# A graph layer of the SAGE kind: gathering rows that are already multiplied by the weights

## The chip, the cores and the metric

One core of one Trainium2 chip runs the whole program. The metric is device time in microseconds (us). The kernel before takes 2383.64 us, the median of 3 runs (2382.04 to 2386.07).

## The reference

Four graph layers follow one another on x, 3327 nodes by 512 features, with one adjacency matrix `adj` (0 or 1). Layers 0, 2 and 3 are graph attention; layer 1 is of the SAGE kind. In front of each layer stands a layer norm and a ReLU, and its result is added to x.

```python
h = jnp.maximum(_layernorm(x, axis=-1), 0.0)
x = x + L1(h, adj, ...)
# L1:
mask = (adj > 0).astype(x.dtype)
deg = jnp.sum(mask, axis=1, keepdims=True)
agg = mask @ x / jnp.maximum(deg, 1.0)
self_f = x @ W_self + b_self
nb_f = agg @ W_nb + b_nb
out = jnp.concatenate([self_f, nb_f], axis=-1) @ W_comb + b_comb
return relu(out)
```

The adjacency is sparse, and nodes of low number have many more neighbours than those of high number (the chance of an edge falls with the root of both numbers).

Layer 1 can be written as relu(h Ws + (mask h / deg) Wn + b), where Ws and Wn are the two weights already multiplied with the halves of W_comb, and b is the sum of the biases. Both kernels compute Ws, Wn and b beside layer 0, and use them (`Wx[:, 0]` and `Wx[:, 1]`, `bias`).

## The kernel before

The nodes lie in 26 blocks of 128. Each block has two groups of 64 nodes. For every group, `PLAN` lists how many tiles of 128 source rows it takes: so many dense ones (the first d blocks of the node table, in order) and so many gathered ones (rows of any number, collected in lists). A dense tile is fetched by a direct DMA on SP's queue; a gathered tile by an indirect DMA which POOL issues (`gather`, L1314). Over all groups there are 77 dense and 291 gathered tiles. Blocks come in the order 0, 24, 1, 23, 2, 22 and so on, a heavy one and a light one in turn, with 12 and 25 last.

Layer 1 has two stages.

In the first, a loop over pairs of blocks, `normed` (L1759 to 1779) turns the output of layer 0 into x1 (batch norm, ReLU and residual), then into h (layer norm and ReLU), which stays in SBUF in `y` and is written to `h_dram`. `own` (L1781 to 1790) turns h by four transposes on PE, copies the result to hT on ACT, multiplies it with Ws by four matmuls, and DVE adds the bias and writes the sum back to `y`.

In the second, blocks are worked on in the order above. Their tiles are taken in parts: one part holds up to two tiles (`SUNIT`) of each of a block's two groups. `load` brings a part's rows into `z_rows` (8 buffers of two tiles, so four parts) and the matching mask to float on ACT. PE multiplies each tile with its mask, 64 columns for each of the two groups, into `sage_acc`, a PSUM tile of [128, 512] (two buffers). When a block's last part is done, `ending` (L1803 on) is started; `tick` moves it a step on at each further part:

1. ACT scales sage_acc by 1/deg into s_ag (L1805);
2. PE transposes it (L1809), ACT copies it to aT (L1811);
3. PE multiplies aT with Wn into n_ps (L1815), and x1's block is fetched;
4. DVE adds y (L1820), then ReLU and residual (L1821), and the block goes to x2. `proj.begin` hands it to the projection of layer 2.

That projection (`Following`, L808 on) runs in the same `tick`: a layer norm, transposes (p_ps), a product with layer 2's weight (p_wh), some small operations, a row of `table2` to DRAM, a last small transpose (p_tr). The attention of layer 2 begins when all of table2 is written.

The program's engines each run their instructions in order. The order within an engine is set by the scheduler when the program is built; SP's queue carries all direct DMAs, POOL's the indirect ones. An indirect gather may read any row, so it waits for the whole of `h_dram`; a direct load waits only for the blocks that it reads.

The functions that the change touches, with the line numbers of the profile:

Of the kernel before, what the change touches and what calls it, by code (L numbers as in the profile page):

```python
# [23 lines left out]
F32 = mybir.dt.float32  # L24
# [9 lines left out]
ALU = mybir.AluOpType  # L34
ET = mybir.EngineType
AX = mybir.AxisListType
PSUM = bass.MemoryType.PSUM
DRAM = bass.MemoryType.DRAM

P = 128  # L40
H = 8
F = 64
D = H * F
KC = D // P
# [26 lines left out]
UNIT = 3  # L71
SLOTS = 2
AHEAD = 3
EPARTS = 5
SUNIT = 2
SROWS = 8
# [1200 lines left out]
def sparse(ctx: ExitStack, tc: tile.TileContext, t: dict, out: bass.AP, WA, ls, cs, idx, rdeg, first):  # L1277
# [5 lines left out]
    nc = tc.nc  # L1283
    N = out.shape[0]
    NP = t["x"].shape[0]
    NB = NP // P
# [5 lines left out]
    dram = ctx.enter_context(tc.tile_pool(name="fdram", bufs=1, space=DRAM))  # L1292
# [8 lines left out]
    mask = keep.tile([P, ls.nm, GB], U8, name="mask")  # L1301
    edges_dram = dram.tile([P, ls.ne, P], BF16, name="edges_dram")

    def take(dst, src, rows):

        n = sum(d for _, d, _ in rows)
        if n:
            c = rows[0][2]
            nc.sync.dma_start(dst[:, :n, :], src[c * P : (c + n) * P, :].rearrange("(k p) w -> p k w", p=P))
        for i, (_, _, k) in enumerate(rows[n:]):  # L1310
            gather(dst[:, n + i, :], src, k)

    def gather(dst, src, k):
        nc.gpsimd.indirect_dma_start(  # L1314
            out=dst, out_offset=None, in_=src[:, :], in_offset=bass.IndirectOffsetOnAxis(ap=idx[:, k : k + 1], axis=0)
        )


    def attend(layer, table, r_dram, r3, finish, tick=lambda: None, home=None, beside=None, edges=None):
# [14 lines left out]
        with tc.tile_pool(name=f"fatt{layer}", bufs=2) as ap, tc.tile_pool(  # L1334
# [164 lines left out]
            spread(0)  # L1499
            for i in range(AHEAD):  # L1500
                load(i)
# [13 lines left out]
            def parts(i):  # L1515

                if layer == 2 and i < EPARTS:
                    for u in range(PG):
                        mine = slice(u * GB, (u + 1) * GB)
                        cut = slice(i * ls.used[u] // EPARTS, (i + 1) * ls.used[u] // EPARTS)  # L1520
                        nc.sync.dma_start(edges[mine, cut, :], edges_dram[mine, cut, :])
# [10 lines left out]
            for i, (j, g, e, rows, s0, begins, stops, last_slots) in enumerate(units):  # L1532
                n, m0 = len(rows), rows[0][0]
                gt = loaded.pop(i).bitcast(F32)
                T = gt[:, :n, H * (F + 1) : ROW]
                load(i + AHEAD)
                parts(i + 1)
# [104 lines left out]


    wx_dram = dram.tile([2, KC, P, D], F32, name="wx_dram")
    h_dram = dram.tile([NP, D], F32, name="h_dram")
    with ExitStack() as mx:
        mid = mx.enter_context(tc.tile_pool(name="fmid", bufs=1))

        y = mid.tile([P, NB, D], F32, name="bn_y")
        bias = mid.tile([P, D], F32, name="sage_b")  # L1650
# [94 lines left out]
        Wx = Wxs[0]  # L1745
        gp = mx.enter_context(tc.tile_pool(name="fsage", bufs=2))
        gps = mx.enter_context(tc.tile_pool(name="fsage_ps", bufs=2, space=PSUM))
        sps = mx.enter_context(tc.tile_pool(name="fsage_n", bufs=1, space=PSUM))
        two = [P, 2, D]
        with tc.tile_pool(name="fln", bufs=1) as bp:  # L1750
            gam = bp.tile([P, D], F32, name="gam")
            bet = bp.tile([P, D], F32, name="bet")
            nc.sync.dma_start(gam, t["L0_gnn_gamma"].partition_broadcast(P))
            nc.sync.dma_start(bet, t["L0_gnn_beta"].partition_broadcast(P))
            nc.vector.tensor_tensor(gam, gam, rsqrt(nc, bp, cs, var, bufs=1)(), ALU.mult)
            nc.vector.tensor_tensor(mean, mean, gam, ALU.mult)
            nc.vector.tensor_tensor(bet, bet, mean, ALU.subtract)

            def normed(c):  # L1759
                xr = bp.tile(two, F32, name="bn_x", tag="bn_x", bufs=3)  # L1760
                nc.sync.dma_start(xr, t["x"][c * P : (c + 2) * P, :].rearrange("(k p) o -> p k o", p=P))
                yy = y[:, c : c + 2, :]
                nc.vector.tensor_tensor(yy, yy, gam.unsqueeze(1).to_broadcast(two), ALU.mult)
                nc.vector.tensor_tensor(yy, yy, bet.unsqueeze(1).to_broadcast(two), ALU.add)
                nc.vector.scalar_tensor_tensor(xr, yy, 0.0, xr, ALU.max, ALU.add)
                nc.sync.dma_start(x1[c * P : (c + 2) * P, :].rearrange("(k p) o -> p k o", p=P), xr)
                mv = bp.tile([P, 2, nc.vector.BN_AGGR_DIM], F32, name="ln_mv", tag="ln_mv", bufs=3)
                for i in range(2):
                    st = bp.tile([P, nc.vector.BN_STATS_DIM], F32, name="ln_st", tag="ln_st", bufs=3)
                    nc.vector.bn_stats(st, xr[:, i, :])  # L1770
                    nc.vector.bn_aggr(mv[:, i, :], st)
                r = rsqrt(nc, bp, cs, mv[:, :, 1:2].rearrange("p k o -> p (k o)"))()
                if c + 2 == NB:
                    nc.vector.tensor_tensor(r[:, 1:2], r[:, 1:2], cs["real"], ALU.mult)
                ng = bp.tile([P, 2, 1], F32, name="ln_ng", tag="ln_ng", bufs=3)
                nc.vector.scalar_tensor_tensor(ng, mv[:, :, 0:1], -1.0, r.unsqueeze(2), ALU.mult, ALU.mult)
                for i in range(2):
                    nc.scalar.activation(yy[:, i, :], xr[:, i, :], AF.Relu, scale=r[:, i : i + 1], bias=ng[:, i, :])
                nc.sync.dma_start(h_dram[c * P : (c + 2) * P, :].rearrange("(k p) o -> p k o", p=P), yy)

            def own(c):  # L1781
                tp = gps.tile([P, KC, P], F32, name="h_ps", tag="a_ps")
                for kc in range(KC):
                    nc.tensor.transpose(tp[:, kc, :], y[:, c, kc * P : (kc + 1) * P], cs["ident"])
                hT = bp.tile([P, KC, P], F32, name="hT", tag="hT", bufs=2)
                nc.scalar.copy(hT, tp)  # L1786
                ps = gps.tile([P, D], F32, name="s_ps", tag="sage_acc")
                for kc in range(KC):
                    nc.tensor.matmul(ps, hT[:, kc, :], Wx[:, 0, kc, :], start=(kc == 0), stop=(kc == KC - 1))  # L1789
                nc.vector.tensor_tensor(y[:, c, :], ps, bias, ALU.add)  # L1790

            for c in range(0, NB, 2):
                normed(c)
                for i in range(2):
                    if c:
                        own(c - 2 + i)
            for i in range(2):
                own(NB - 2 + i)

        proj = following(mx, 2, 1, t["L2_gnn_W"], 3, 2, (t["L2_gnn_a1"], t["L2_gnn_a2"]))  # L1800
        ends = []

        def ending(b, acc):  # L1803
            ag = gp.tile([P, D], F32, name="s_ag", tag="s_ag")
            nc.scalar.mul(ag, acc, rdeg[:, b : b + 1])  # L1805
            yield
            tp = gps.tile([P, KC, P], F32, name="a_ps", tag="a_ps")
            for kc in range(KC):
                nc.tensor.transpose(tp[:, kc, :], ag[:, kc * P : (kc + 1) * P], cs["ident"])  # L1809
            aT = gp.tile([P, KC, P], F32, name="aT", tag="aT")  # L1810
            nc.scalar.copy(aT, tp)  # L1811
            yield
            ps = sps.tile([P, D], F32, name="n_ps", tag="n_ps")
            for kc in range(KC):
                nc.tensor.matmul(ps, aT[:, kc, :], Wx[:, 1, kc, :], start=(kc == 0), stop=(kc == KC - 1))  # L1815
            xr = gp.tile([P, D], F32, name="fsage_x", tag="sage_x", bufs=3)
            nc.sync.dma_start(xr, x1[b * P : (b + 1) * P, :])
            yield
            o = gp.tile([P, D], F32, name="s_o", tag="s_o", bufs=3)
            nc.vector.tensor_tensor(o, ps, y[:, b, :], ALU.add)  # L1820
            nc.vector.scalar_tensor_tensor(o, o, 0.0, xr, ALU.max, ALU.add)  # L1821
            nc.sync.dma_start(x2[b * P : (b + 1) * P, :], o)
            proj.begin(b, o)
# [9 lines left out]
        def batches(g):  # L1833
            rows = ls.rows(g)
            return [rows[k : k + SUNIT] for k in range(0, len(rows), SUNIT)]

        for b in ls.order:
            ps = list(zip_longest(*(batches(b * PG + u) for u in range(PG))))
# [3 lines left out]
        def load(i):  # L1842
            if i >= len(parts):
                return
            zs = loaded[i] = []
            for u, rows in enumerate(parts[i][1]):
                if rows is not None:
                    n, m0 = len(rows), rows[0][0]
                    zt = gp.tile([P, SUNIT, D], F32, name="z_rows", tag="z_rows", bufs=SROWS)
                    mf = gp.tile([P, SUNIT, GB], F32, name="z_mask", tag="z_mask", bufs=SROWS)  # L1850
                    nc.scalar.copy(mf[:, :n, :], mask[:, m0 : m0 + n, :])  # L1851
                    take(zt, h_dram, rows)
                    for k in range(n):
                        zs.append((k, u, m0 + k, mf[:, k, :], zt[:, k, :]))
            zs.sort(key=lambda x: x[:2])

        for i in range(SAHEAD):
# [1 line left out]
        for i, (b, _, begins, stops) in enumerate(parts):  # L1859
            load(i + SAHEAD)  # L1860
            if begins:
                acc = gps.tile([P, D], F32, name="sage_acc", tag="sage_acc")
# [120 lines left out]
```

## Time and profile before

| | us |
|---|---|
| median of 3 runs | 2383.64 |
| the profiled execution's own time | 2389.36 |
| its span, from the first to the last instruction | 2387.6 |
| PE busy in the span | 1868.2 (78%) |
| DVE busy | 1706.4 (71%) |
| POOL busy | 1162.9 (49%) |
| ACT busy | 1110.2 (47%) |
| DMA | 577.63 MB, mean 242 GB/s |
| layer 1, first stage (first transposes to last product) | 859.6 to 970.9 |
| layer 1, second stage (to the last gathered tile) | 970.9 to 1366.9 |
| first gather of layer 2 | 1395.1 |

The mean granted TensorE clock was 0.870. A line of a timeline has the start, the duration, the engine, the source line, the operation, what it writes and reads, and the count; in square brackets stands the idle time of the engine before it and what ended that, where "issue" is time in which the engine waited for nothing that the profile shows. A PE matmul in float32 shows as two records. Releasers are inferred, and a wait for several things is put down to the one that came last.

### The profile page before, as it was taken

To read this page: it belongs to the slowest core of one execution; us is meant where nothing else is said; L and a number is where in the kernel's file an instruction comes from. 1 tells how busy PE (TensorE), PEld (TensorE's weight loads), DVE (VectorE), ACT (ScalarE), POOL (GpSimd) and SP (SyncE) were. 2 spreads that over 40 slices of the span, in tenths; PEclk is the share of its full clock that TensorE was granted. 3 is DMA by queue.
4 is the path that set the end of the run, shared out by engine and by line. 5 is a ranking of instruction groups with operands and counts; after the bars stand their busy time and mean duration, and the time that the engine had idled before them with its cause. 6 is when DMAs were issued, how large, how long until landed. Compare 5 with 4: busy or idle time off the path is not lost. (4 is left out here: it accounts for less than half of the span.)

```text
span 2387.6 us, 43165 instructions
## 1 busy us (share of the span) xinstructions
PE 1868.2 (78%) x14899; PEld 1042.4 (44%) x14899; DVE 1706.4 (71%) x3061; ACT 1110.2 (47%) x4149; POOL 1162.9 (49%) x1227
## 2 busy tenths in 40 slices
PE   5888416897888869899999936888888857776875
PEld 4554204454555424333333324555444435444442
DVE  5455866788989895044445549878787749999996
ACT  3566101455666633133333312577796822445543
POOL 1000013476777500477776435655655335776762
PEclk9887757899999979999999968888898966779777
DMA  6676118798889665689888688877787548888883
GB/s 274 245 291 225 42 39 299 264 316 287 270 261 295 197 247 189 216 280 307 292 287 296 219 248 272 246 246 227 235 253 223 155 182 260 271 278 259 278 287 118
DMA packets 213728, 577.63 MB, mean 242 GB/s; under 512 B 37838, under 2 KB 44076, under 8 KB 210174
## 3 DMA queue, kind: packets, MB, share of 16 engines
q0 software_dynamic: 93504, 328.25, 43.6%
q1 hardware_dynamic: 119998, 246.53, 29.8%
q8 instruction: 121, 1.98, 0.3%
q14 instruction: 105, 0.86, 0.1%
HBM read 511.41 MB, written 63.25 MB: 241 GB/s over the span
## 5 line engine op out<-in xcount | busy, mean ns | idle before, releaser
L1314 POOL DMA_INDIRECT rows_e<-table,idx x654 | 625.9, 957 | 363.0 <-issue 148.3
L1577 PE MATMUL facc<-vw,ones_of 128*64 128x260 f32 x2616 | 447.2, 457 | 78.5 <-DVE vw L1543 61.0
L1588 PE MATMUL facc<-rows_s,wgt 128*64 128x65 f32 x7200 | 343.9, 247 | 170.8 <-DVE wgt L1557 115.8
L1588 PEld LDWEIGHTS facc<-rows_s,wgt 128*64 128x64 f32 x7200 | 289.8, 156 | 291.2 <-DVE wgt L1557 147.7
L1543 DVE TENSOR_TENSOR vw<-rows_e,w_of 128x1040 f32<-128x1040 f32 (+1 forms) x270 | 395.6, 1465 | 9.6 <-DVE w_of L1540 0.2
L1314 POOL DMA_INDIRECT z_rows<-h_dram,idx x291 | 278.8, 958 | 237.0 <-issue 156.3
L1314 POOL DMA_INDIRECT rows_s<-table,idx x219 | 211.1, 964 | 239.1 <-PE facc L1588 142.9
L1553 DVE TENSOR_TENSOR mx<-r_bc,rows_s 128x1024 f32<-128x1024 f32 (+1 forms) x255 | 280.4, 1100 | 46.6 <-DMA rows_s<-table 34.1
L1557 DVE TENSOR_TENSOR wgt<-mx,mask 128x1024 f32<-128x1024 f32 (+1 forms) x255 | 280.3, 1099 | 38.4 <-ACT mask L1455 20.9
L1404 ACT ACTIVATE fhp<-sums,rd 64x64 f32<-64x64 f32 x816 | 215.6, 334 | 185.3 <-DVE rd L1397 182.1
L1577 PEld LDWEIGHTS facc<-vw,ones_of 128*64 128x64 f32 x2616 | 195.4, 156 | 225.7 <-issue 94.2
L1867 PE MATMUL sage_acc<-z_rows,z_mask 128*64 128x512 f32 x736 | 188.7, 611 | 11.5 <-DMA z_rows<-h_dram 5.9
L1218 POOL DMA_DIRECT2D list_b<-shift x8 | 4.0, 513 | 325.3 <-DVE shift L1179 325.3
L1820 DVE TENSOR_TENSOR s_o<-n_ps,bn_y 128x512 f32<-128x512 f32 x26 | 18.0, 692 | 150.2 <-PE n_ps L1815 141.8
L1851 ACT CAST z_mask<-mask 128x128 f32<-128x128 uint8 (+1 forms) x201 | 52.5, 284 | 154.4 <-PE sage_acc L1867 154.0
L741 PE MATMUL wh_ps<-fWt,hT 128*128 128x512 f32 x208 | 121.5, 738 | 0.0
L1391 ACT COPY sums<-facc 128x260 f32<-128x260 f32 x153 | 56.1, 367 | 140.5 <-PE facc L1577 139.3
L1404 ACT ACTIVATE bn_y<-sums,rd 64x64 f32<-64x64 f32 x408 | 107.7, 334 | 2.9 <-DVE rd L1397 1.3
L1495 DVE TENSOR_REDUCE w_of<-r_of 128x16 f32<-128x48 f32 (+1 forms) x270 | 61.4, 227 | 62.1 <-PE r_of L1487 35.9
L1867 PEld LDWEIGHTS sage_acc<-z_rows,z_mask 128*64 128x64 f32 x736 | 51.4, 137 | 114.8 <-issue 94.0
L1789 PE MATMUL s_ps<-fWx,hT 128*128 128x512 f32 x208 | 93.9, 605 | 5.1 <-ACT hT L1786 5.1
L1455 ACT ACTIVATE mask<-on 128x128 uint8<-128x128 uint16 (+1 forms) x85 | 25.2, 297 | 153.3 <-DVE on L1433 151.0
(260 smaller groups left out, 3006.8 us busy)
## 6 DMA issues: line engine op xcount, KB each, us to landing
adj_i<-in_adj SPq DMA_DIRECT2D x26, 1664.0 KB
rows_s<-table SPq DMA_DIRECT2D x46, 528.0 KB
table<-v_row SPq DMA_DIRECT2D x78, 264.0 KB
rows_s<-table SPq DMA_DIRECT2D x62, 264.0 KB
rows_s<-table SPq DMA_DIRECT2D x23, 632.0 KB
fin_x<-fx SPq DMA_DIRECT2D x52, 256.0 KB
z_rows<-h_dram SPq DMA_DIRECT2D x23, 512.0 KB
rows_e<-table,idx POOLq DMA_INDIRECT x654
```

The costliest lines, as they stand in the source:

```text
L741: nc.tensor.matmul(wh, hT[:, kc, :], self.Wt[:, kc, :], start=(kc == 0), stop=(kc == KC - 1))
L1314: nc.gpsimd.indirect_dma_start(out=dst, out_offset=None, in_=src[:, :], in_offset=bass.IndirectOffsetOnAxis(ap=idx[:, k : k + 1], axis=0))
L1391: nc.scalar.copy(sm, accs.pop(g)[:, :sw])
L1404: nc.scalar.mul(hp[o0 : o0 + GB, h * F : (h + 1) * F], sm[mine, q, 0:F], rd[mine, q, :])
L1495: nc.vector.tensor_reduce(w[:, :n], re[:, :n].rearrange("p k (t h) -> p k h t", h=H), AX.X, ALU.add)
L1543: nc.vector.tensor_tensor(vw[:, :n], gt[:, :n, : H * (F + 1)].rearrange("p k (h x) -> p k h x", x=F + 1), w[:, :n].unsqueeze(3).to_broadca ...
L1553: nc.vector.tensor_tensor(mx[:, :n], rbs[j].unsqueeze(1).to_broadcast(full), T.unsqueeze(3).to_broadcast(full), ALU.max)
L1557: nc.vector.tensor_tensor(wt[:, :n], mx[:, :n], mk.unsqueeze(2).to_broadcast(full), ALU.mult)
L1577: nc.tensor.matmul(accs[g][v * GB : (v + 1) * GB, :sw].rearrange("p (q x) -> p q x", x=F + 1), ones_of[i][:, k, :], by[:, v], start=f, stop=l,
L1588: nc.tensor.matmul(accs[g][v * GB : (v + 1) * GB, q * (F + 1) : (q + 1) * (F + 1)], wt[:, k, h, :], gt[:, k, h * (F + 1) : (h + 1) * (F + 1)],
L1789: nc.tensor.matmul(ps, hT[:, kc, :], Wx[:, 0, kc, :], start=(kc == 0), stop=(kc == KC - 1))
L1867: nc.tensor.matmul(acc[u * GB : (u + 1) * GB, :], m, z, start=f, stop=l)
```

## The change

mask h Wn is the same as mask (h Wn). The changed kernel multiplies first and gathers then.

- In the first stage `own` is replaced by two steps. `turn(c)` transposes h and copies it back to `y`, over h itself. `sent(c)` multiplies the turned h with Wn, and ACT copies the product z to SBUF, from where it goes to `z_dram`. `sent` is one block behind `turn`, and the loop runs four block numbers longer. There is no `h_dram` any more.
- In the second stage, the gathered rows are rows of z. `ending` has two steps in place of four: four matmuls of the turned h in `y` with Ws into n_ps, and then on DVE the bias, sage_acc times 1/deg, and ReLU and residual. The scaling on ACT, the four transposes and the copy aT are gone.
- z of blocks 0 and 1 is written to a tile `hot` in SBUF (and from there to z_dram). `load` doesn't fetch these two blocks' dense tiles: PE reads them from `hot`. That holds for 57 of the 77 dense tiles. A buffer of `z_rows` is still assigned to such a part.
- n_ps has two PSUM buffers instead of one; a_ps is gone.

```diff
+HOT = 2
-    def take(dst, src, rows):
+    def take(dst, src, rows, skip=0):
         n = sum(d for _, d, _ in rows)
-        if n:
-            c = rows[0][2]
-            nc.sync.dma_start(dst[:, :n, :], src[c * P : (c + n) * P, :].rearrange("(k p) w -> p k w", p=P))
+        if n > skip:
+            c = rows[skip][2]
+            nc.sync.dma_start(dst[:, skip:n, :], src[c * P : (c + n - skip) * P, :].rearrange("(k p) w -> p k w", p=P))
...
-                nc.sync.dma_start(h_dram[c * P : (c + 2) * P, :].rearrange("(k p) o -> p k o", p=P), yy)
-
-            def own(c):
-                tp = gps.tile([P, KC, P], F32, name="h_ps", tag="a_ps")
+
+            def turn(c):
+                tp = gps.tile([P, KC, P], F32, name="h_ps", tag="n_ps")
                 for kc in range(KC):
                     nc.tensor.transpose(tp[:, kc, :], y[:, c, kc * P : (kc + 1) * P], cs["ident"])
-                hT = bp.tile([P, KC, P], F32, name="hT", tag="hT", bufs=2)
-                nc.scalar.copy(hT, tp)
-                ps = gps.tile([P, D], F32, name="s_ps", tag="sage_acc")
+                nc.scalar.copy(y[:, c, :].rearrange("p (k o) -> p k o", o=P), tp)
+
+            def sent(c):
+                ps = gps.tile([P, D], F32, name="z_ps", tag="sage_acc")
                 for kc in range(KC):
-                    nc.tensor.matmul(ps, hT[:, kc, :], Wx[:, 0, kc, :], start=(kc == 0), stop=(kc == KC - 1))
-                nc.vector.tensor_tensor(y[:, c, :], ps, bias, ALU.add)
-
-            for c in range(0, NB, 2):
-                normed(c)
+                    nc.tensor.matmul(ps, y[:, c, kc * P : (kc + 1) * P], Wx[:, 1, kc, :], start=(kc == 0), stop=(kc == KC - 1))
+                if c < HOT:
+                    z = hot[:, c, :]
+                else:
+                    z = bp.tile([P, D], F32, name="z_out", tag="z_out", bufs=3)
+                nc.scalar.copy(z, ps)
+                nc.sync.dma_start(z_dram[c * P : (c + 1) * P, :], z)
+
+            for c in range(0, NB + 4, 2):
+                if c < NB:
+                    normed(c)
                 for i in range(2):
-                    if c:
-                        own(c - 2 + i)
-            for i in range(2):
-                own(NB - 2 + i)
+                    if 0 <= c - 2 < NB:
+                        turn(c - 2 + i)
+                    if 0 <= c - 3 + i < NB:
+                        sent(c - 3 + i)
...
         def ending(b, acc):
-            ag = gp.tile([P, D], F32, name="s_ag", tag="s_ag")
-            nc.scalar.mul(ag, acc, rdeg[:, b : b + 1])
-            yield
-            tp = gps.tile([P, KC, P], F32, name="a_ps", tag="a_ps")
-            for kc in range(KC):
-                nc.tensor.transpose(tp[:, kc, :], ag[:, kc * P : (kc + 1) * P], cs["ident"])
-            aT = gp.tile([P, KC, P], F32, name="aT", tag="aT")
-            nc.scalar.copy(aT, tp)
-            yield
-            ps = sps.tile([P, D], F32, name="n_ps", tag="n_ps")
-            for kc in range(KC):
-                nc.tensor.matmul(ps, aT[:, kc, :], Wx[:, 1, kc, :], start=(kc == 0), stop=(kc == KC - 1))
             xr = gp.tile([P, D], F32, name="fsage_x", tag="sage_x", bufs=3)
             nc.sync.dma_start(xr, x1[b * P : (b + 1) * P, :])
+            ps = gps.tile([P, D], F32, name="n_ps", tag="n_ps")
+            for kc in range(KC):
+                nc.tensor.matmul(ps, y[:, b, kc * P : (kc + 1) * P], Wx[:, 0, kc, :], start=(kc == 0), stop=(kc == KC - 1))
             yield
             o = gp.tile([P, D], F32, name="s_o", tag="s_o", bufs=3)
-            nc.vector.tensor_tensor(o, ps, y[:, b, :], ALU.add)
+            nc.vector.tensor_tensor(o, ps, bias, ALU.add)
+            nc.vector.scalar_tensor_tensor(o, acc, rdeg[:, b : b + 1], o, ALU.mult, ALU.add)
             nc.vector.scalar_tensor_tensor(o, o, 0.0, xr, ALU.max, ALU.add)
...
-                    take(zt, h_dram, rows)
+                    held = sum(d and c < HOT for _, d, c in rows)
+                    take(zt, z_dram, rows, held)
                     for k in range(n):
-                        zs.append((k, u, m0 + k, mf[:, k, :], zt[:, k, :]))
+                        zs.append((k, u, m0 + k, mf[:, k, :], hot[:, rows[k][2], :] if k < held else zt[:, k, :]))
```

More of the change, by code (lines that the diff above doesn't have):

```diff
@@ L1644, in sparse @@
     wx_dram = dram.tile([2, KC, P, D], F32, name="wx_dram")
-    h_dram = dram.tile([NP, D], F32, name="h_dram")
+    z_dram = dram.tile([NP, D], F32, name="z_dram")
     with ExitStack() as mx:
@@ L1747, in sparse @@
         gps = mx.enter_context(tc.tile_pool(name="fsage_ps", bufs=2, space=PSUM))
-        sps = mx.enter_context(tc.tile_pool(name="fsage_n", bufs=1, space=PSUM))
+        hot = mx.enter_context(tc.tile_pool(name="fhot", bufs=1)).tile([P, HOT, D], F32, name="hot")
         two = [P, 2, D]
```

## The prediction

> **What bounds the kernel now.** I read the page's timeline first: between about 840 and 1400 us no matrix of edges is weighed any more, and this is the only stretch that the diff touches. Then I cut that stretch by its ends and asked for the busy time of each piece. Columns: stretch, its length, then busy us (instructions) of PE, PE's weight loads, DVE, ACT and POOL, granted clock, DMA share, GB/s.
>
> ```profile
> 859.60:970.90 111.30, 106.16 (x314) 51.76 (x314) 71.67 (x160) 37.09 (x73) 1.91 (x2) 0.98 0.58 203
> 970.90:1011.00 40.10, 29.75 (x99) 9.91 (x98) 0.69 (x1) 7.15 (x25) 25.49 (x27) 0.91 0.88 308
> 1011.00:1366.90 355.90, 354.75 (x1242) 133.72 (x1242) 167.59 (x355) 127.55 (x618) 251.36 (x263) 1.00 0.86 282
> 1366.90:1395.10 28.20, 17.78 (x48) 7.82 (x47) 16.57 (x38) 9.12 (x48) 0.00 (x0) 0.90 0.49 144
> ```
>
> Row 1 is the loop of `normed` and `own`, row 2 the first blocks of gathered rows, row 3 the rest of them, row 4 the way to the next attention. PE fills 354.75 of 355.90 us in row 3. But POOL, at 251.36, is nearly as full as it can be. The timeline of POOL shows why:
>
> ```profile
> 933.98 0.96 POOL L1314 DMA_INDIRECT z_rows<-h_dram,idx  x1 [98.10 <-issue]
> 935.24 0.95 POOL L1314 DMA_INDIRECT z_rows<-h_dram,idx  x1 [0.30 <-issue]
> 973.13 0.94 POOL L1314 DMA_INDIRECT z_rows<-h_dram,idx  x1 [36.93 <-PE sage_acc L1867]
> 974.38 0.94 POOL L1314 DMA_INDIRECT z_rows<-h_dram,idx  x1 [0.30 <-issue]
> ...
> 1010.08 0.94 POOL L1314 DMA_INDIRECT z_rows<-h_dram,idx  x1 [4.22 <-PE sage_acc L1867]
> ...
> 1350.68 0.94 POOL L1314 DMA_INDIRECT z_rows<-h_dram,idx  x1 [0.30 <-issue]
> ```
>
> A gather takes 0.95 us and the next starts 0.30 later even with nothing to wait for: 1.25 us each. From 973.13 to 1350.68 there are 288 such steps, 360 us of 377.6, so POOL has 17.5 us of real waiting, some 6 of it before 1017 us. PE's own order in one late block:
>
> ```profile
> 1351.35 0.60 PE L915 MATMUL p_ps<-fident,ln_h 128*128 128x128 f32 x4
> 1351.88 1.94 PE L1867 MATMUL sage_acc<-z_rows,z_mask 128*64 128x512 f32 x8
> 1353.75 0.28 PE L947 MATMUL p_tr<-fident,r_half 128*16 128x128 f32 x1
> 1353.86 3.60 PE L923 MATMUL p_wh<-fWt,hT 128*128 128x512 f32 x8
> 1357.39 1.94 PE L1867 MATMUL sage_acc<-z_rows,z_mask 128*64 128x512 f32 x8
> 1359.26 0.66 PE L1809 MATMUL a_ps<-fident,s_ag 128*128 128x128 f32 x4
> 1359.85 1.94 PE L1867 MATMUL sage_acc<-z_rows,z_mask 128*64 128x512 f32 x8
> 1361.72 3.70 PE L1815 MATMUL n_ps<-fWx,aT 128*128 128x512 f32 x8
> 1365.25 0.60 PE L915 MATMUL p_ps<-fident,ln_h 128*128 128x128 f32 x4
> ```
>
> From start to start a block is 13.90 us: 5.6 for twelve gathered tiles (two halves run side by side, so 0.93 a pair), 3.53 for n_ps, 4.2 for the next layer's projection, and 0.59 for the four transposes of L1809. The same block has 10 gathers, 12.5 us of POOL. So two engines are within 10% of each other; PE leads by little.
>
> **What the skill says.** The Trainium skill, Perfetto Trace Analysis, section What "DMA-bound" means, lists as a case of its own the sequencer of the issuing engine being solid with DMA slices, whose window is descriptor generation and not data movement. The trace agrees: the step of 1.25 us does not move whether the DMA share is 0.86 or 0.91. The change alters neither the number (291) nor the shape of the gathers. GPSIMD Engine Reference, section Key points, says POOL shares its SBUF interfaces with VectorE when that has two SBUF inputs; the added DVE operations have one in PSUM and one in SBUF, and the trace, whose DVE is busy half of this time, has a median gather of 946 ns against a shortest of 940, so I cost this at nothing. DMA: Bandwidth & Descriptors, section Anatomy of one DMA, gives a transfer 2.0 us plus bytes/436e3; I use it below, once.
>
> **The change part by part.**
>
> *First loop (L1762 to 1800).* PE keeps 104 transposes and 104 matmuls of 512 columns. In the changed order of instructions they alternate by block (4 transposes, 4 matmuls, the matmuls one block behind), where before it was two blocks at a time. Before, PE waited 5.1 us over 12 times for the copy hT; the copy now has a batch of matmuls (3.5 us) to hide behind, against which alternating costs 26 x (0.59 - 0.52 + 0.04) = 2.9 us. I take 2.5 us gained: PE ends at 968.4 instead of 970.9. Bounds: 5 gained to 10 lost. ACT gets 26 copies z of 0.58 us, 15 us on an engine busy 37 of 111; DVE loses 26 additions of 0.69. ACT is in order and waits up to 3.9 us for DVE's normalization (L1776); behind it stand both copies that PE needs, which the batch of matmuls covers.
>
> *The start of the gathers.* This is what the change makes later. h_dram was whole at 929 us, so 7 direct loads and 2 gathers (16 of block 0's 39 tiles) lay in SBUF when PE came at 970.9. z_dram is whole only after PE's last product: 968.4 + 0.6 copy + 0.4 issue + 3.4 landing = 972.8. For the landing the skill gives 2.6 us for 256 KB as an estimate; the trace has 4.57 from the issue at 929.41 to the gather at 933.98 for twice the bytes; I take 3.4. POOL's queue, 973.13 before, thus starts at the same time but owes two gathers more, 2.5 us. The order of SP keeps 5 direct loads inside the loop, and hot rows give 4 tiles, so 14 of 39 tiles are there. What block 0 and block 24 still have to load is the same: 25 + 8 tiles against 23 + 10. The loads of ab and fWt (1.5 MB) stand ahead of the direct loads as before. PE fills its first hole with the own products of block 0, which need no gather. Bounds: 0 to 8 us lost.
>
> *Transposes, scaling and aT gone.* PE loses 26 x 0.59 = 15.3 us. ACT loses 52 operations of 0.6; DVE gains 26 of 0.69 (it is busy 168 of 356). Both have room.
>
> *Hot rows.* 57 direct loads of a 256 KB tile vanish, 14.9 MB; at 282 GB/s that is 53 us of transfers. They go by SP's queue, not by POOL's; PE's waits for direct loads were 5.9 us in two waits, both at the start. I cost the gain at nothing, with a bound of 6 us.
>
> *The sum.* PE needs 384.5 - 15.3 = 369.2 us from 968.4: 1337.6 if never idle. POOL needs 291 x 1.25 = 363.8 from 972.8: 1336.6, and a landing. Two lines of the same length that must follow each other block by block add up to more than either. So I step through the blocks in their order: POOL advances 1.25 x gathers; PE's end of a block is the later of (its last end + 0.93 a pair + 3.53 + 4.15) and (last gather + 3.5). With POOL held 6 us early on, as measured, this gives for the kernel before (with 0.59 more a block and its own starts) 1365.3, where the trace has 1366.9. For the changed kernel it gives 1006 for block 0, 1157 for block 5, 1237 for block 8, 1276 for block 15 and 1355.8 at the end: PE waits for POOL in the heavy first blocks, and leads again in the last ten. Gain 9.5 us, not 15.3.
>
> *The end.* The last block before:
>
> ```profile
> 1366.90 0.70 ACT L1805 ACTIVATE s_ag<-sage_acc,rdeg 128x512 f32<-128x512 f32 x1
> 1370.97 0.58 ACT L1811 COPY aT<-a_ps 128x512 f32<-128x512 f32 x1 [2.59 <-PE a_ps L1809]
> 1375.35 0.69 DVE L1820 TENSOR_TENSOR s_o<-n_ps,bn_y 128x512 f32<-128x512 f32 x1 [0.75 <-PE n_ps L1815]
> 1376.08 0.69 DVE L1821 SCALAR_TENSOR_TENSOR s_o<-s_o,fsage_x 128x512 f32<-128x512 f32 x1
> ```
>
> The result is there at 1376.8, 9.9 us after the last gathered tile. After the change, the own products follow on PE (3.6), then three DVE operations (0.2 + 2.1): 5.9. Gain 4.0. What follows, up to the first gather of the next layer at 1395.11, hangs on this and moves with it.
>
> Total 9.5 + 4.0 = 13.5, rounded to 14. The profiled execution took 2389.4 with a span of 2387.6; the median of the runs is 2383.64. Span about 2373.6, median 2369.6.
>
> **The rivals.** *Gather queue not held at the start:* if fewer transfers spare POOL its 6 us, the stepping gives 1349.8 and the gain is 20: about 2363. For it: 14.9 MB less; against: hardly any less before 1016. *A worse start:* PE stands with nothing loaded, 6 to 10 us more than I count: gain 4 to 8, about 2377. For it: the gathers need all of z_dram; against: PE waited through that time before, too. *Transfers are the bound:* 53 us less, about 2331; for it a DMA share of 0.86, against it PE's 354.75 of 355.90 and POOL's fixed step. *Slower:* in the first loop ACT doesn't keep up with the alternation, and PE stands through both copies of each block: 26 x 1.16 = 30 us, some 16 lost in all, about 2400. It decides from 0.6 us of waiting a block. Against it: a batch of matmuls lasts 3.5 us, and ACT is a third busy.
>
> **How the numbers follow.** The forecast as stated 0.62 (2365 to 2375), unheld queue 0.15, worse start 0.13, transfers 0.03, slower 0.07. The range 2358 to 2378 leaves out the last two and part of the third. 0.2% is 4.8 us, about what a measurement of this kernel can tell from none. Faster 0.89, within it 0.05 (the worst of the bad starts), slower 0.06.
>
> **What would show it.** POOL's steps stay 1.25 us with about 291 of them ending near 1340 to 1345; PE's busy share of 1011 to 1350 falls below 0.98, with waits for indirect z_rows in blocks 1 to 6; the first loop ends by 969; 5.9 us from the last gathered tile to the result; DMA share near 0.75. I am wrong if PE waits for ACT in each block of the first loop, if the first gather starts after 977, or if POOL still waits as long for PE as before.

## The result and the profile after

The changed kernel takes 2362.35 us (median of 6 runs, 2356.1 to 2369.05) beside 2384.36 us for the kernel before (6 runs, 2382.04 to 2391.02): ratio 0.9904, with a 95% interval of 0.9882 to 0.9927. That is 22 us faster, 17 to 28 by the interval, where 14 were forecast. Its profiled execution took 2360.66 us with a span of 2358.9, and the mean granted clock was 0.868 (0.870 before). The profiled execution of the kernel before, 2389.36 us, is longer than five of its six runs, so the two profiles lie further apart than the medians.

The same four pieces of the layer in the profile after. The outer cuts lie at the same events as before; the cut between rows 2 and 3 is a round time, so these two rows are compared as a sum. Columns as before: stretch, length, then busy us of PE, PE's weight loads, DVE, ACT and POOL, granted clock, DMA share, GB/s.

```profile
853.75:958.57 104.82, 104.05 (x312) 51.20 (x313) 55.57 (x135) 49.64 (x98) 0.00 (x0) 0.97 0.58 198
958.57:1000.00 41.43, 33.11 (x100) 9.89 (x100) 4.14 (x9) 6.68 (x25) 25.62 (x27) 0.92 0.77 259
1000.00:1349.80 349.80, 345.14 (x1150) 125.07 (x1148) 184.13 (x380) 109.05 (x574) 254.12 (x264) 1.00 0.82 255
1349.80:1374.30 24.50, 13.83 (x36) 5.84 (x35) 12.73 (x31) 7.03 (x41) 0.00 (x0) 0.87 0.62 174
```

The first loop fell from 111.3 to 104.8 us, the second stage (rows 2 and 3) from 396.0 to 391.2, the way to the next gather (row 4) from 28.2 to 24.5. Together the layer is 535.5 - 520.6 = 14.9 us shorter. The spans differ by more, 28.7 us. The other 13.8 lie where the diff changes nothing: 5.9 ahead of the layer (it begins at 853.75 instead of 859.60) and 7.9 after it (984.6 from the first gather of layer 2 to the end, 992.5 before).

**The gathers.** The timeline of POOL after, from the first gather to the last and on to layer 2:

```profile
962.49 0.96 POOL L1315 DMA_INDIRECT z_rows<-z_dram,idx  x1 [132.49 <-PE sage_acc L1867]
963.76 0.96 POOL L1315 DMA_INDIRECT z_rows<-z_dram,idx  x1 [0.31 <-issue]
...
981.38 0.95 POOL L1315 DMA_INDIRECT z_rows<-z_dram,idx  x1 [4.12 <-PE sage_acc L1867]
...
1337.70 0.94 POOL L1315 DMA_INDIRECT z_rows<-z_dram,idx  x1 [0.30 <-PE sage_acc L1867]
1374.30 0.95 POOL L1315 DMA_INDIRECT rows_e<-table,idx  x1 [35.66 <-ACT ones_of L1454]
```

The step is still 1.25 us. The first gather comes 3.9 us after PE's last product (958.57), and the last starts 375.2 us later. 290 steps of 1.25 are 362.5 of these, so POOL is 97% full. That is nearer than before, when 288 steps filled 360 of 377.6 us, to the sequencer case that the prediction took from the Trainium skill (Perfetto Trace Analysis, What "DMA-bound" means). But PE is as full, 345.14 of 349.80 us in row 3.

**The loop.** PE's timeline in the loop after, two blocks (start, duration, engine, line, operation, records):

```profile
861.07 0.60 PE L1784 MATMUL h_ps<-fident,bn_y 128*128 128x128 f32 x4
861.50 3.60 PE L1790 MATMUL z_ps<-fWx,bn_y 128*128 128x512 f32 x8
864.94 0.60 PE L1784 MATMUL h_ps<-fident,bn_y 128*128 128x128 f32 x4
865.38 3.60 PE L1790 MATMUL z_ps<-fWx,bn_y 128*128 128x512 f32 x8
```

The same timeline in the kernel before, one pair of blocks:

```profile
879.91 7.13 PE L1789 MATMUL s_ps<-fWx,hT 128*128 128x512 f32 x16 [0.24 <-ACT hT L1786]
886.88 1.04 PE L1784 MATMUL h_ps<-fident,bn_y 128*128 128x128 f32 x8
888.16 7.13 PE L1789 MATMUL s_ps<-fWx,hT 128*128 128x512 f32 x16 [0.24 <-ACT hT L1786]
```

After, the starts are 3.87 us apart per block, so a pair is 7.74, against 8.25 before. Four transposes that follow matmuls directly delay the next matmul by 0.43 us here, not by their 0.60.

**One late block and the end.** PE's timeline after, the counterpart of the block shown before:

```profile
1311.12 3.70 PE L1815 MATMUL n_ps<-fWx,bn_y 128*128 128x512 f32 x8
1314.66 0.60 PE L916 MATMUL p_ps<-fident,ln_h 128*128 128x128 f32 x4
1315.19 1.08 PE L1867 MATMUL sage_acc<-hot,z_mask 128*64 128x512 f32 x4
1316.10 1.03 PE L1867 MATMUL sage_acc<-z_rows,z_mask 128*64 128x512 f32 x4
1317.06 0.28 PE L948 MATMUL p_tr<-fident,r_half 128*16 128x128 f32 x1
1317.17 3.60 PE L924 MATMUL p_wh<-fWt,hT 128*128 128x512 f32 x8
1320.70 3.65 PE L1867 MATMUL sage_acc<-z_rows,z_mask 128*64 128x512 f32 x16
1324.29 1.12 PE L1815 MATMUL n_ps<-fWx,bn_y 128*128 128x512 f32 x2
```

From n_ps to n_ps it is 13.17 us with the same twelve tiles (24 records; two of the tiles are dense and ten gathered) and one projection; it was 13.90. The transposes of L1809 are gone and nothing took their place. The last tile and the last block's result, on PE and DVE:

```profile
1347.03 2.79 PE L1867 MATMUL sage_acc<-z_rows,z_mask 128*64 128x512 f32 x10
1349.75 3.70 PE L1815 MATMUL n_ps<-fWx,bn_y 128*128 128x512 f32 x8
...
1353.48 0.69 DVE L1818 TENSOR_TENSOR s_o<-n_ps,sage_b 128x512 f32<-128x512 f32 x1 [2.29 <-PE n_ps L1815]
1354.21 0.75 DVE L1819 SCALAR_TENSOR_TENSOR s_o<-sage_acc,rdeg,s_o 128x512 f32<-128x512 f32 x1
1355.00 0.69 DVE L1820 SCALAR_TENSOR_TENSOR s_o<-s_o,fsage_x 128x512 f32<-128x512 f32 x1
```

The result is there at 1355.7, 5.9 us after the last tile (9.9 before); the next gather follows 18.6 later (18.3 before).

### The profile page after: what moved, and what is told of

Its sections match the earlier page's. It is cut to its first block, busy times and chain, and to the rows that moved or that the text cites. A ratio compares the mean times of both kernels' runs of the same rounds, so it can differ in the third digit from the quotient of the medians.

```text
span 2358.9 us, 42783 instructions
## 1 busy us (share of the span) xinstructions
PE 1853.9 (79%) x14795; PEld 1033.1 (44%) x14795; DVE 1703.4 (72%) x3061; ACT 1102.6 (47%) x4123; POOL 1167.0 (49%) x1227
## 3 DMA queue, kind: packets, MB, share of 16 engines
HBM read 496.47 MB, written 63.25 MB: 237 GB/s over the span
## 5 line engine op out<-in xcount | busy, mean ns | idle before, releaser
L1589 PE MATMUL facc<-rows_s,wgt 128*64 128x65 f32 x7200 | 349.1, 249 | 166.5 <-DVE wgt L1558 112.4
L1589 PEld LDWEIGHTS facc<-rows_s,wgt 128*64 128x64 f32 x7200 | 294.9, 159 | 286.6 <-DVE wgt L1558 140.6
L1315 POOL DMA_INDIRECT z_rows<-z_dram,idx x291 | 279.7, 961 | 228.9 <-PE sage_acc L1867 154.1
L1867 PE MATMUL sage_acc<-z_rows,z_mask 128*64 128x512 f32 x622 | 165.4, 604 | 13.0 <-DMA z_rows<-z_dram,idx 12.8
L1818 DVE TENSOR_TENSOR s_o<-n_ps,sage_b 128x512 f32<-128x512 f32 x26 | 18.0, 692 | 167.0 <-PE n_ps L1815 163.3
L1815 PE MATMUL n_ps<-fWx,bn_y 128*128 128x512 f32 x208 | 97.3, 610 | 0.0
L1352 PE MATMUL r_bc<-r_two,fones 2*128 2x512 f32 x156 | 85.3, 547 | 14.4 <-DMA r_two<-r_dram 8.8
L924 PE MATMUL p_wh<-fWt,hT 128*128 128x512 f32 x208 | 96.0, 605 | 0.3 <-ACT hT L919 0.3
```

What stands on the lines that cost most here:

```text
L924: nc.tensor.matmul(wh, hT[:, kc, :], self.Wt[:, kc, :], start=(kc == 0), stop=(kc == KC - 1))
L1315: nc.gpsimd.indirect_dma_start(out=dst, out_offset=None, in_=src[:, :], in_offset=bass.IndirectOffsetOnAxis(ap=idx[:, k : k + 1], axis=0))
L1352: nc.tensor.matmul(rb, ones[0:2, :].bitcast(F32R), rrs.pop(j).bitcast(F32R), start=True, stop=True)
L1589: nc.tensor.matmul(accs[g][v * GB : (v + 1) * GB, q * (F + 1) : (q + 1) * (F + 1)], wt[:, k, h, :], gt[:, k, h * (F + 1) : (h + 1) * (F + 1)],
L1815: nc.tensor.matmul(ps, y[:, b, kc * P : (kc + 1) * P], Wx[:, 0, kc, :], start=(kc == 0), stop=(kc == KC - 1))
L1867: nc.tensor.matmul(acc[u * GB : (u + 1) * GB, :], m, z, start=f, stop=l)
```

## The experiments

The theory is the prediction's: the layer gains where PE loses work, and PE and POOL lead in turn. The rivals are that only one of the two sets the pace, that the start of the gathers does, or that the hot rows do.

The runs were made on three chips, called A, B and C here. There the kernel before takes 2692, 2659 and 2657 us, 11 to 13% more than above, so that the chip of the first pair is taken to be another one ("the first chip" below). Each ratio is to the kernel before on the same chip. Stretches of the layer are cut as above, in us of one profile, and single profiles scatter by about 10 us in each large part. The last column sums PE's idle stretches of over 1 us in the second stage; they are called holds below. The one profile of after_third is of its longest execution (2657.87 us, where the median is 2636.85), so no stretch of it is compared.

| chip, kernel | ratio to before | first loop | second stage | to next gather | PE idle, > 1 us |
|---|---|---|---|---|---|
| first pair: before | | 111.3 | 396.0 | 28.2 | 11.1 |
| first pair: after | 0.9904 | 104.8 | 391.2 | 24.5 | 8.6 |
| A: before_again | 0.9999 | 111.4 | 474.9 | 29.6 | 64.5 |
| A: lag_only | 0.9981 | 102.5 | 466.2 | 30.2 | 55.7 |
| A: hot_only | 0.9993 | 111.5 | 470.1 | 28.7 | 60.7 |
| A: after_again | 0.9873 | 105.3 | 443.8 | 24.9 | 38.9 |
| B: no_hot | 0.9899 | 104.9 | 447.8 | 26.7 | 38.0 |
| B: early | 0.9860 | 104.4 | 452.2 | 22.5 | 58.5 |
| B: pe_back | 0.9875 | 104.6 | 459.0 | 25.2 | 54.3 |
| B: relief_after | 0.9640 | 105.5 | 382.8 | 25.1 | 8.2 |
| C: after_third | 0.9896 | - | - | - | - |
| C: pe_back_2 | 0.9881 | 104.8 | 449.9 | 25.1 | 43.4 |
| C: deep | 0.9906 | 104.5 | 441.4 | 24.6 | 48.8 |
| C: relief_before | 0.9776 | 111.4 | 410.9 | 28.2 | 22.5 |

**Both kernels again.** before_again is the kernel before unchanged; after_again and after_third are the changed kernel unchanged.

> The kernel before once more, for the spread of one execution's stages. Theory (two engines share the bound, and the layer's own stretch is what changed): from the first transposes of layer 1 to the first gather of layer 2 again 535.5 us within 1, while the stretches before and after it, whose code is the same in both kernels, scatter by several us. Rival (something outside of layer 1 also got faster with the change): the stretches outside are again those of the first profile of before, 859.6 and 992.5 us, within 2.

> The changed kernel once more. Theory: layer 1's stretch again 520.5 us within 1, and the ratio to before between 0.990 and 0.995, of which 0.9937 is layer 1's 15 us. Rival (something outside got faster too): ratio at or below 0.990, with the stretches outside at 853.8 and 984.6 us within 2 again.

> The changed kernel as it is, so that the other runs of this call have it on their own chip. If the gain is the same share everywhere: ratio to before 0.987 to 0.991. If it hangs on how fast the chip serves the gathers: near 0.990 where the kernel before takes 2384 us, near 0.987 where it takes 2690.

Measured: 0.9999 (0.9975 to 1.0024), 0.9873 (0.9824 to 0.9922) and 0.9896 (0.9868 to 0.9924). The gain as a share is the same on all chips within the intervals. Where it lies is not: the layer, expected at 535.5 and 520.5 us again, took 615.9 and 574.0 on chip A. The windows of the first loop and the second stage in before_again, on chip A:

```profile
955.40:1066.80 111.40, 106.02 (x312) 51.71 (x312) 71.63 (x160) 37.00 (x73) 1.92 (x2) 0.98 0.58 203
1066.80:1541.70 474.90, 404.94 (x1340) 150.78 (x1340) 168.01 (x356) 134.87 (x643) 275.67 (x289) 0.92 0.75 238
```

And in after_again, on the same chip:

```profile
946.70:1052.00 105.30, 104.22 (x314) 51.25 (x314) 55.57 (x135) 49.50 (x98) 0.00 (x0) 0.97 0.58 197
1052.00:1495.80 443.80, 396.74 (x1249) 140.33 (x1248) 187.06 (x388) 109.52 (x597) 279.96 (x291) 0.95 0.71 225
```

The loop is as long here as on the first chip. The second stage is 79 us longer in the kernel before and 53 in the changed one, and the change shortens it by 31 us where the first pair has 4.8. PE was busy 354.75 of 355.90 us in the late rows on the first chip; here it stands still 70 of 474.90. The timeline of before_again, of several engines, has two kinds of moment:

```profile
1136.37 1.23 DVE L926 TENSOR_TENSOR sd_pr<-p_wh,ab 128x1024 f32<-128x1024 f32 x1 [8.50 <-remote]
...
1136.50 0.50 ACT L1851 CAST z_mask<-mask 128x128 f32<-128x128 uint8 x2 [9.71 <-remote]
1136.73 0.94 POOL L1314 DMA_INDIRECT z_rows<-h_dram,idx  x1 [3.02 <-remote]
...
1158.36 0.66 PE L1809 MATMUL a_ps<-fident,s_ag 128*128 128x128 f32 x4
...
1169.75 0.59 ACT L1811 COPY aT<-a_ps 128x512 f32<-128x512 f32 x1 [6.03 <-remote]
1170.39 5.75 PE L1815 MATMUL n_ps<-fWx,aT 128*128 128x512 f32 x8 [9.51 <-issue]
...
1212.29 0.59 ACT L1811 COPY aT<-a_ps 128x512 f32<-128x512 f32 x1 [5.42 <-remote]
1212.93 6.66 PE L1815 MATMUL n_ps<-fWx,aT 128*128 128x512 f32 x8 [8.54 <-issue]
```

In the first, three engines with different work go on within 0.4 us of each other: DVE after 8.5 us, ACT after 9.7, POOL after 3.0. "remote" is the profile's word where it sees a wait end and finds no releaser among the program's engines. In the second ACT stands still, and PE stands for the copy aT; PE's next eight records then take 5.75 and 6.66 us, where 3.70 is usual (the granted clock was 0.50 from 1165 to 1171). No engine has a stretch of "issue" or "remote" over 1 us in the second stage of either kernel on the first chip.

The trace says more of what ends these waits. In it an engine tells the others of finished work by counting up a semaphore, and the copy aT at 1169.75 starts 0.02 us after PE counted up its own (at 1169.73; the count before came at 1155.61). But by PE's records the transposes that it copies had ended at 1159.02, 10.7 us earlier. DVE, ACT and POOL at 1136 wait for the same semaphore of PE. On the first chip aT starts at most 0.49 us after the end of its transposes, in all 26 blocks; here six of 26 start 3.9 to 10.7 us after it with ACT idle. So these look like waits for PE's word that a product is done. Whether that word comes late or PE's records run ahead of its work stays open, also because the trace of before_again holds only 425 of the 575 such counts of this stage (574 on the first chip).

Chip A has three kernels with the old ending (before_again, lag_only, hot_only). On average their second stage is 470.4 us, with 60.3 of idle stretches and 403.0 busy on PE; after_again has 443.8, 38.9 and 396.7. So of 26.6 us, 6.3 are PE's work, as much as on the first chip (384.50 - 378.25), and 21.4 are shorter holds of PE (small gaps give 1 back). That PE is held less because its waits for s_ag and aT are gone fits the lines: five of before_again's holds, 28.8 of its 64.5 us, stand at n_ps<-aT, which the changed kernel doesn't have. But no run puts these two ACT steps back alone, so it isn't shown.

**The order of the loop alone.** The kernel before, with each block's products one block behind its transposes:

```diff
-            def own(c):
+            hTs = {}
+
+            def turn(c):
...
-                hT = bp.tile([P, KC, P], F32, name="hT", tag="hT", bufs=2)
+                hT = hTs[c] = bp.tile([P, KC, P], F32, name="hT", tag="hT", bufs=3)
...
+            def own(c):
+                hT = hTs.pop(c)
...
-            for c in range(0, NB, 2):
-                normed(c)
+            for c in range(0, NB + 4, 2):
+                if c < NB:
+                    normed(c)
...
-                    if c:
-                        own(c - 2 + i)
-            for i in range(2):
-                own(NB - 2 + i)
+                    if 0 <= c - 2 < NB:
+                        turn(c - 2 + i)
+                    if 0 <= c - 3 + i < NB:
+                        own(c - 3 + i)
```

> The kernel before, with the products of its first loop one block behind the transposes, as in the changed kernel, and nothing else. Theory: the first loop falls from 111.3 to about 105 us, and the whole by 6 us. Rival (the loop got shorter because DVE lost its additions and ACT writes in place): it stays at 110 to 111, and the time is as before.

Measured: 0.9981 (0.9959 to 1.0003), and the loop in its profile is 102.5 us instead of 111.4. PE's timeline has the rhythm of the changed kernel:

```profile
980.45 0.60 PE L1786 MATMUL h_ps<-fident,bn_y 128*128 128x128 f32 x4
980.89 3.60 PE L1794 MATMUL s_ps<-fWx,hT 128*128 128x512 f32 x8
984.32 0.60 PE L1786 MATMUL h_ps<-fident,bn_y 128*128 128x128 f32 x4
```

3.87 us per block, and no wait for hT is left. So the alternating order, not the rest of the change, is what shortens the loop. The whole program's interval, down to 11 us, agrees with the 8.9 but can't confirm it.

**The hot rows, alone and taken away.** hot_only is the kernel before with rows of h of blocks 0 and 1 kept in SBUF; no_hot is the changed kernel with all dense tiles loaded.

```diff
+                if c == 0:
+                    nc.scalar.copy(hot, yy)
...
-                    take(zt, h_dram, rows)
+                    held = sum(d and c < HOT for _, d, c in rows)
+                    take(zt, h_dram, rows, held)
```

```diff
-HOT = 2
+HOT = 0
```

> The kernel before, with h of the first two blocks copied to SBUF once and read from there, and nothing else. Theory (transfers are not the bound): the DMA share of the second stage falls from 0.86 to about 0.75, the time by 0 to 4 us, all of it in the first 50 us of the stage. Rival (transfers hold PE up): 10 us or more less.

> The changed kernel without the hot blocks: all 77 dense tiles are loaded. Theory (transfers are not the bound): 0 to 4 us over the changed kernel, at the start of the second stage. Rival (transfers hold PE up): 10 us or more over it.

Measured: hot_only 0.9993 (0.9972 to 1.0014), no_hot 0.9899 (0.9850 to 0.9948) beside 0.9873 and 0.9896 with hot rows. The profile after has 14.9 MB less read from HBM (496.47 MB, 511.41 before), but the time hardly shows it: hot_only gains 2 us by its middle and at most 8 by its interval. The changed kernel with hot rows and without them ran on different chips; by the middles hot rows are worth 1 to 7 us in it, and the intervals allow for no gain as well as for 15 us.

**An early start of the gathers.** The changed kernel, gathering from x1, which is whole much sooner (so the aggregate is of rows of x1):

```diff
-                    take(zt, z_dram, rows, held)
+                    take(zt, x1, rows, held)
```

> The changed kernel, but the tiles of the second stage are fetched from x1, whole 40 us earlier, in place of z_dram (which is still written); so the aggregate is of other rows. Theory (the late start of the gathers costs PE some 10 us of waiting, which two engines in line can't make good): from the last product to the last gathered tile 381 to 385 us in place of 391.2. Rival (PE alone sets the stage, waits at the start are filled later): 389 to 391.

Measured: 0.9860 (0.9802 to 0.9918). Its first gather in POOL's timeline:

```profile
1007.10 0.96 POOL L1315 DMA_INDIRECT z_rows<-fx,idx  x1 [85.54 <-DMA z_dram<-z_out]
```

That is 43 us before the end of its loop at 1049.7; in after_again the first gather comes at 1055.9, 3.9 us after the loop. The ratio is not distinguishable from no_hot's on the same chip (10 us less, give or take 20), and the second stage is no shorter (452.2 against 447.8). A start 40 us earlier shows no gain on this chip, but a gain of the 6 to 10 us that the prediction's rival is about would not be seen.

**Four transposes back on PE.** The changed kernel with four transposes a block added to `ending`, whose result nobody reads; run on two chips:

```diff
+            tp = gps.tile([P, KC, P], F32, name="d_ps", tag="d_ps", bufs=1)
+            for kc in range(KC):
+                nc.tensor.transpose(tp[:, kc, :], y[:, b, kc * P : (kc + 1) * P], cs["ident"])
```

> The changed kernel with four transposes per block put back into the ending, whose result nobody reads: PE's removed work alone comes back, 15.3 us. Theory (two engines share the bound): 8 to 12 us over the changed kernel. Rival (PE alone sets it): 15. Rival (POOL sets it): under 3.

> The changed kernel with four transposes per block put back on PE, whose result nobody reads: 26 x 0.59 = 15.3 us more of PE's time in the second stage. If PE sets the pace: 12 to 16 us longer than the changed kernel on the same chip, ratio higher by 0.005 to 0.007. If the prediction's stepping is right (two engines in turn): 8 to 11 us. If POOL sets the pace: under 5 us.

Measured: 0.9875 (0.9825 to 0.9924) and 0.9881 (0.9821 to 0.9942). On chip C the changed kernel has 0.9896. The difference is -4 us, give or take some 18 by the two intervals, so no cost is seen, but a cost of 12 us, the least that was expected if PE alone sets the pace, is not excluded. The profile on C has 579.8 us for the layer, against 570.5 in deep (below), no more than two profiles differ by. The two runs don't decide between the theories.

**One gather in four replaced.** In both kernels, every fourth gathered tile comes by a direct load of some block instead (so the aggregate is of other rows); every byte is still moved, and POOL has 218 steps instead of 291.

```diff
-            gather(dst[:, n + i, :], src, k)
+            if spare and k % 4 == 0:
+                c = k % NB
+                nc.sync.dma_start(dst[:, n + i, :], src[c * P : (c + 1) * P, :])
+            else:
+                gather(dst[:, n + i, :], src, k)
```

> The changed kernel, but one gathered tile in four is a direct load of a whole block by SP's queue, of the same size; so POOL issues about 73 gathers fewer and the aggregate is of other rows. Theory (POOL's fixed step of 1.25 us holds PE up in the heavy blocks): PE's waits after 1000 us, 4.7 us, and some of the 8.3 before it go, and the stage falls by 5 to 10 us. Rival (PE alone sets it): by 1 or less beyond the start. Rival (POOL alone sets it): by 40 us or more.

> The kernel before, with one gather in four replaced by a direct load of some block (so the aggregate is of other rows): POOL has 218 steps instead of 291, 91 us less to issue, and every byte is still moved. Theory of the prediction (PE leads by little before the change): the second stage, 396 us in the first profile, can fall only to PE's own need of 384.5, so 5 to 12 us less, ratio 0.995 to 0.998. Rival (the gathers set the pace before the change too, as the run of the changed kernel with this relief had it): 40 to 70 us less, ratio 0.970 to 0.985.

Measured: 0.9640 (0.9587 to 0.9693) for the changed kernel, 0.9776 (0.9717 to 0.9836) for the kernel before. The window of the second stage in relief_before:

```profile
1048.40:1459.30 410.90, 386.50 (x1340) 145.15 (x1340) 168.44 (x356) 134.93 (x643) 207.54 (x217) 0.97 0.81 275
```

And in relief_after:

```profile
1049.20:1432.00 382.80, 371.47 (x1249) 134.68 (x1248) 187.02 (x389) 112.87 (x599) 207.59 (x218) 0.98 0.78 261
```

Whole runs: 59.5 us less than the kernel before on chip C, and on chip B 69 us less than no_hot (0.9640 against 0.9899). By the profiles the second stage falls by as much, from 447.8 (no_hot) to 382.8 on one chip; relief_before's 410.9 has only the 470.4 of chip A to stand beside. So on these chips 73 gathers cost some 60 us in both kernels, and the prediction's "PE leads by little", by which 5 to 12 us could be gained, doesn't hold there before the change. But POOL's queue was not full: 291 steps of 1.25 us are 364 of 470.4 us, 77%, and 81% of no_hot's stage. PE's holds fall from 60.3 to 22.5 us and from 38.0 to 8.2, and its busy time by 16.5 and 28 us, while its granted clock over the stage rises from 0.92 to 0.97 and from 0.95 to 0.98. So the holds come with the gathers. The run changes three things at once, POOL's work, the queue that carries the rows and the order in which rows are read; which of them counts, and how it delays PE's word to ACT and DVE, is open. On the first chip, which had none of the late waits, no relief was run, so what a gather is worth there is open too.

**More buffers.** The changed kernel with `SROWS` 10 instead of 8, so ten buffers of two tiles in z_rows:

```diff
-SROWS = 8
+SROWS = 10
```

> The changed kernel with ten tile buffers in z_rows instead of eight, so five parts may be under way. If POOL is held by buffers that PE has not yet released (4.1 and 1.2 us at the start, 1.4 later in the profile after), the second stage gets 3 to 8 us shorter than in the changed kernel, 1 to 3 per mille. If POOL's own step of 1.25 us is what sets the pace, nothing: within 2 us. If a landing later than usual is what PE waits for, more parts under way help most on a slow chip: 10 to 30 us.

Measured: 0.9906 (0.9873 to 0.9939) beside 0.9896 for eight buffers on the same chip. A further part under way shows no gain; the second stage of its profile, 441.4 us, is within the scatter of the other profiles with the new ending (443.8 to 459.0).

## Why the prediction was right or wrong

- **First loop: right in sign, too small.** Forecast 2.5 us gained, measured 6.5. The term that was off is 26 x (0.59 - 0.52 + 0.04) = +2.9 for alternating, against 5.1 us of waits. It took the transposes at about their own duration. In the traces the alternating pair is 7.74 us and the old pair without its wait 8.25 - 0.24 = 8.01, so alternating saves 13 x 0.27 = 3.5 us on top of the waits. lag_only shows 8.9, near 5.1 + 3.5. Of this the changed kernel keeps 6.5. Its loop is 2.3 us longer than that of lag_only at two places: its one wait for ACT's copy costs 1.0, and its first products take 5.64 us instead of 4.44, with the granted clock at half until 5.8 us into the loop instead of 3.3. The rival "ACT can't keep up" needed 0.6 us of waiting a block: the trace has that one wait, 0.77 us, in the whole loop.
- **The start of the gathers: right.** The first gather stands 3.9 us behind PE's end (forecast 4.4), and PE's largest wait there is 5.45 us. Waits of over 1 us at the start sum to 8.6, less than the 10.0 before, so the rival of a worse start falls on the first chip; the early run is too coarse to say more. (The prediction's 929 us for a whole h_dram is the time when its last write was issued, 929.41; its first gather began at 933.98.)
- **A gather queue not held at the start: not what happened.** The measured 2362 lies next to this rival's 2363, but by chance. POOL's waits for PE in its first 55 us, beyond its own step, fell from 6.7 to 4.7 us and not to nothing, and the layer gained 14.9 us, not 20.
- **Transposes, scaling and aT gone, and the stepping: right in direction, mechanism not confirmed.** The 9.5 up to the last gathered tile held 2.5 of the loop, so the second stage was to fall by 7.0; it fell by 4.8. The mechanism was that PE waits for POOL in the heavy first blocks. PE's share of the late window was to fall below 0.98; it is 345.14 of 349.80, 0.987, and after 1010 us the waits are five of 0.33 to 0.79 us, 3.0 together. So PE leads almost throughout, and POOL, which filled 375.2 us against a forecast of 367 to 372, keeps up just behind it. What POOL's time holds beyond its steps is still 12.7 us, where it was 17.5. So it is not waiting for POOL that keeps the gain small. What ate PE's gain is seen when the stage is summed by tile: a_ps is gone with 16.4 us, but p_wh has 192 records instead of 184 in this stretch, 3.6 us more. One block's projection that used to run after the last gathered tile now runs before it (36 records instead of 48 on PE after it, four of the twelve being the transposes). The rest are 1.6 us more in sage_acc, 1.2 in n_ps, 1.5 more of idle time, and some 3 that the transposes had shared with their neighbours: their own sum overstated what they cost.
- **Hot rows at nothing: not contradicted.** hot_only has 2 us by its middle, and every interval allows for no gain at all, though also for more than the bound of 6 us. The DMA share is 0.82 in the late window, not the 0.75 expected. The rival "transfers are the bound", 53 us, falls.
- **The end: right to the tenth** for the result (5.9 against 9.9). The way from it to the next gather didn't stay quite the same (18.6 against 18.3), so 3.7 arrive.
- **The total: near for the layer, partly by luck.** 13.5 were summed for the layer and 14.9 are measured in it, because the loop gained 4.0 more than forecast and the second stage 2.2 less. The 22 us of the medians are 7 more than the layer. The profiles have 13.8 us outside of it, where the code is the same; 6.7 of these only say that the two profiles lie further apart than the medians. The cause of the rest is not settled. On chip A nothing of the kind is seen: there the parts outside of the layer sum to 2081.1, 2087.4 and 2082.3 us in the three kernels with the old ending and to 2085.4 in after_again, while the layer alone gives 41.9, more than the 34 us of the ratio.

## What to carry to other kernels

A short operation between long ones of the same engine can cost less than its duration, as the transposes did here: read its price from the starts of what stands on either side, in the order that the change will have. When the chain of steps after the last tile gets shorter, look for work that was hidden in its holes; here a projection didn't vanish but moved ahead of the last tile. A stage in which PE hardly waits on one chip can be full of holds on another, so measure an experiment beside its own kernel before, and read which part of the gain is work and which is waiting.

## What the runs showed of the hardware

- The same program took 11 to 13% longer on chips A, B and C than for the first pair. The step of a gather stayed 1.25 us, the first loop 111.4 us, and the stage of gathers grew from 396 to 475 us (chip A).
- In that stage, on chip A, ACT began to copy PE's finished transposes up to 10.7 us after PE's record of them had ended; on the first chip it was at most 0.49 us. PE's first batch after such a hold took 5.4 to 6.8 us instead of 3.7 (n_ps in before_again).
- 73 indirect gathers less, with the same bytes moved by direct loads, shortened that stage by 60 to 65 us, 0.8 to 0.9 us for each, though POOL's steps had filled only 77 to 81% of it.
- Four transposes of 0.60 us between two batches of float32 matmuls delayed the second by 0.43 us.
